# Rotary queries and keys of a two-layer decoder, produced with their dimensions on partitions

## The chip, the cores and the metric

The kernel runs on one core of one Trainium2 chip, as a single launch. The metric is the device time of that launch in microseconds. The median of three runs of the kernel before is 1182.6 us (1182.31 to 1185.84).

## The reference

Eight sequences (B) of 256 tokens (S) with 256 features (D) pass through two decoder layers, all in float32. Every layer is self-attention, cross-attention and a feed-forward network of experts, each on a layer norm of the residual stream and added back to it. Only the self-attention is touched by the change. It has 16 heads of 16 dimensions. Layer 0, cut to what matters:

```python
def _rotate_half(x):                      # layer 0: pairs of neighbours
    x1 = x[..., 0::2]
    x2 = x[..., 1::2]
    return jnp.stack((-x2, x1), axis=-1).reshape(x.shape)
...
q = (x @ Wq.T + bq).reshape(B, S, H, D).transpose(0, 2, 1, 3)
k = (x @ Wk.T + bk).reshape(B, S, H, D).transpose(0, 2, 1, 3)
v = (x @ Wv.T + bv).reshape(B, S, H, D).transpose(0, 2, 1, 3)
q = q * cos + _rotate_half(q) * sin       # _apply_rope
k = k * cos + _rotate_half(k) * sin
attn = jax.nn.softmax(jnp.einsum('bhqd,bhkd->bhqk', q, k) / SCALE, axis=-1)
out = jnp.einsum('bhqk,bhkd->bhqd', attn, v)
return out.transpose(0, 2, 1, 3).reshape(B, S, E) @ Wo.T + bo
```

Layer 1 has no biases, masks the future (causal), and its rotation exchanges the two halves of a head: dimension i goes with dimension i + 8, `concatenate([-t2, t1])`.

## The kernel before

Three stages follow one another: the attention of both layers with layer 0's experts, the projections and cross-attention of layer 1, and layer 1's experts. The change lies in the first stage alone, in the function `plain`.

That stage is a list of 24 *units*, each one attention of one sequence. Counted from 0 in the order in which they run: self-attention of sequences 0 and 1 (units 0, 1), their cross-attention (2, 3), then the same for the next two sequences, up to unit 15; units 16 to 23 are the self-attention of layer 1. The experts of layer 0 (`chosen_experts`, a generator, among it a Sinkhorn chain in which TensorE's `cs` sums alternate with short VectorE instructions) are threaded between the units.

A unit has four *steps* (k = 0 to 3). In step k TensorE makes the next scores (`Core.scores`, L326 to L360: four matmuls into the tile `st`, which fills four PSUM banks and has one buffer), ScalarE turns them into two exponential tiles `pT` (L345), in layer 1 GpSimd zeroes the future in each (`affine_select`, L350), and TensorE multiplies the exponentials of the step before with the values (`o`, L371). VectorE transposes and divides what comes out (`divided_T`, L382).

Everything a unit needs ahead of its first scores is done during the units before it. `beside(n, k, at, made)` puts a piece of work into step k of unit n, after the value products; `EARLY` puts it before them. The order on all five engines is as written (`tc.manual_schedule`), each engine taking its instructions strictly in that order. The pieces of a self-attention unit n are, with their places:

- `norm` (unit n-3, step 3, early) and `rows` (n-2, step 2): the layer norm, and its transposition to `xnT`, features on partitions.
- `heads(0)` (n-2, step 3) and `heads(1)` (n-1, step 0), L452: queries and keys of tokens 0 to 127, then of tokens 128 to 255, side by side in one PSUM tile `qk` of 128 tokens x 512 columns. `product4` (L280) splits each 128x128 stationary operand into four of 32 columns, which write to four bands of 32 partitions. `rotary` (L399) multiplies from PSUM on VectorE: `qc` by the cosine table, and in two instructions `qs`, the exchanged neighbours (or halves) by the sine table. In layer 0 GpSimd adds the rotated bias (`turned`, L457). The sum of `qc` and `qs` goes to `qkr`: for the first half on GpSimd (L459), for the second on VectorE in `joined` (L463; n-1, step 1, early).
- `vals(0)`, `vals(1)` (L465): the values, copied by ScalarE to `padv`.
- `begin` (L470; n-1, step 1): four TensorE transposes of the keys and a ScalarE copy to `kT`; four transposes of the queries to the PSUM tile `qps`, and two ScalarE copies of it with a mask each (`masked_queries`, L309) to `qm`.

The tables `cos`, `sin0`, `sin1` lie with tokens on partitions, one row per token and 16 columns. The biases of queries, keys and output lie in `bs`, one row repeated on all partitions; `turn` (L574) rotates the first two once at the start. Before the loop (L948 to L968) the first units' pieces are issued in an order of their own.

Of the kernel before, what the change touches and what calls it, by code (L numbers as in the profile page):

```python
# [39 lines left out]
P = 128  # L40
# [117 lines left out]
def plain(  # L158
# [37 lines left out]
    bs = wa.tile([P, 3, D], F32, name="bias")  # L196

    def load_bias(i, v):
        row = a[f"L0_attn_{v}"].rearrange("(o d) -> o d", o=1)
        nc.sync.dma_start(bs[:, i, :], row.to_broadcast([P, D]))  # L200

    load_bias(0, "bq")
    load_bias(1, "bk")
# [8 lines left out]
    load_bias(2, "bo")  # L212
# [186 lines left out]
    def rotary(qk, t, layer, work):  # L399

        qc = work.tile([P, 2 * H, HD], F32, tag="qc", name="qc")
        nc.vector.tensor_tensor(
            qc,
            qk.rearrange("p (h d) -> p h d", d=HD),
            cos[:, t, :].unsqueeze(1).to_broadcast([P, 2 * H, HD]),
            ALU.mult,
        )
        qs = work.tile([P, 2 * H, HD], F32, tag="qs", name="qs")
        if layer == 0:
            of = "p (h i s) -> p s h i"  # L410
            src, dst = qk.rearrange(of, s=2, i=HD // 2), qs.rearrange("p h (i s) -> p s h i", s=2)
            sn = sin0[:, t, :].rearrange("p (i s) -> p s i", s=2)
        else:
            of = "p (h s i) -> p s h i"
            src, dst = qk.rearrange(of, s=2, i=HD // 2), qs.rearrange("p h (s i) -> p s h i", s=2)
            sn = sin1[:, t, :].rearrange("p (s i) -> p s i", s=2)
        for s in range(2):
            nc.vector.tensor_tensor(
                dst[:, s],
                src[:, 1 - s],  # L420
                sn[:, s, :].unsqueeze(1).to_broadcast([P, 2 * H, HD // 2]),
                ALU.mult,
            )
        return qc.rearrange("p h d -> p (h d)"), qs.rearrange("p h d -> p (h d)")

    class SelfAttention:
# [17 lines left out]
        def rows(self):  # L444
            self.xnT = transposed(self.xn, work, mm, "xnT")
            self.qkr = work.tile([P, 2, 2 * D], F32, tag="qkr", name="qkr")
# [5 lines left out]
        def heads(self, t):  # L452
            qk = mm.tile([P, 2 * D], F32, tag="mm", name="qk")
            self.projected(qk, t, 0, 2 * D)
            qc, qs = rotary(qk, t, self.layer, work)
            if self.bias is not None:
                nc.gpsimd.tensor_tensor(qc, qc, self.bias[0][:, t, :], ALU.add)  # L457
            if not t:
                nc.gpsimd.tensor_tensor(self.qkr[:, t, :], qc, qs, ALU.add)  # L459
            self.parts = qc, qs  # L460

        def joined(self):
            nc.vector.tensor_tensor(self.qkr[:, 1, :], *self.parts, ALU.add)  # L463
# [6 lines left out]
        def begin(self):  # L470
            kT = transposed(self.qkr[:, :, D:], work, mm, "kT")
            qps = mm.tile([P, 2, S], F32, tag="mm", name="qps")
            for t in range(2):
                for c in range(2):
                    nc.tensor.transpose(qps[:, c, bass.ts(t, P)], self.qkr[:, t, bass.ts(c, P)], ident)
            qm = masked_queries(work, qps, mask2)
            mine = dens[:, 2 * self.layer, 2 * self.b : 2 * self.b + 2]
            self.core = Core(kT, qm, self.v_pad, 1.0 / math.sqrt(HD), self.layer == 1, None, mine)
# [92 lines left out]
    turned = pads.tile([P, 2, 2 * D], F32, name="turned")  # L571
    offset = pads.tile([P, D], F32, name="offset")

    def turn():  # L574
        for t in range(2):
# [393 lines left out]
    for n, u in enumerate(units):  # L969
        if n == 1:  # L970
            expert_tables()
        if n == 3:
            zeros()
# [1886 lines left out]
```

## Time and profile before

| | us |
|---|---|
| median of three runs | 1182.6 |
| the profiled execution | 1187.22 |
| its span, first to last instruction | 1185.5 |
| first scores of unit 0 begin (timeline) | 22.45 |
| scores of the last step of unit 23 begin (timeline) | 446.49 |
| mean granted TensorE clock | 0.993 |

How the clock was granted and how the engines were used in 40 equal slices of 29.6 us each stands on the page:

```profile
PE   5798899998899999999999999999999999999997
...
DVE  5555777777766633833433424242324583222213
ACT  2576665764434451323232323232413231222220
POOL 2335355454736731414141414141416214100004
PEclk8999999999999999999999999999999999999999
```

Each digit is the busy share of a slice in tenths; PEclk is the clock that TensorE was granted, in tenths of full speed. The attention units fill the first fifteen slices. Of a group of instructions the profile gives the time in which at least one of them ran, then the mean of one: four matmuls on four bands of the array run at the same time, so the first number is less than the count times the mean.

### The profile page before, as it was taken

To read this page: it belongs to the slowest core of one execution; us is meant where nothing else is said; L and a number is where in the kernel's file an instruction comes from. 1 tells how busy PE (TensorE), PEld (TensorE's weight loads), DVE (VectorE), ACT (ScalarE), POOL (GpSimd) and SP (SyncE) were. 2 spreads that over 40 slices of the span, in tenths; PEclk is the share of its full clock that TensorE was granted. 3 is DMA by queue.
4 is the path that set the end of the run, shared out by engine and by line. 5 is a ranking of instruction groups with operands and counts; after the bars stand their busy time and mean duration, and the time that the engine had idled before them with its cause. 6 is when DMAs were issued, how large, how long until landed. Compare 5 with 4: busy or idle time off the path is not lost.

```text
span 1185.5 us, 32965 instructions
## 1 busy us (share of the span) xinstructions
PE 1128.8 (95%) x14300; PEld 704.3 (59%) x14300; DVE 565.5 (48%) x1564; ACT 447.5 (38%) x696; POOL 420.9 (36%) x482
## 2 busy tenths in 40 slices
PE   5798899998899999999999999999999999999997
PEld 2344444453445454566666666666666576888864
DVE  5555777777766633833433424242324583222213
ACT  2576665764434451323232323232413231222220
POOL 2335355454736731414141414141416214100004
PEclk8999999999999999999999999999999999999999
DMA  7036233050200600010101020202012107699924
GB/s 228 1 123 217 92 107 106 10 167 1 85 2 12 223 20 3 18 38 19 38 19 41 16 51 6 55 2 55 2 37 75 36 19 319 258 411 394 404 89 140
DMA packets 51451, 116.84 MB, mean 99 GB/s; under 512 B 8273, under 2 KB 36417, under 8 KB 46945
## 3 DMA queue, kind: packets, MB, share of 16 engines
q1 hardware_dynamic: 45120, 98.90, 24.4%
q0 software_dynamic: 3456, 12.73, 3.0%
q10 hardware_dynamic: 2720, 3.02, 0.7%
q8 instruction: 114, 1.87, 0.6%
q14 instruction: 41, 0.33, 0.1%
HBM read 104.00 MB, written 27.93 MB: 111 GB/s over the span
## 4 chain that ended last, share of the span: by engine, by line
PE 76%; DVE 7%; POOL 6%; issue 6%; ACT 4%; DMA 1%; SPq 0%; POOLq 0%; ACTq 0%; DVEq 0%
PE h L276 7%; PE k L276 6%; PE v L276 6%; PE wo L276 5%; PE ox L1471 5%; PE stx L1431 5%; PE st L334 4%; PE out L1848 4%; PE out L1665 4%; PE o L371 3%; PE qk L282 3%; PE h L1079 3%; PE q L276 3%; ACT pT L345 2%; PE tr L291 2%
## 5 line engine op out<-in xcount | busy, mean ns | idle before, releaser
L345 ACT ACTIVATE pT<-st 128x1024 f32<-128x1024 f32 (+1 forms) x128 | 110.7, 920 | 65.1 <-PE st L334 63.9
L371 PE MATMUL o<-pT,padv 128*32 128x256 f32 (+1 forms) x1536 | 99.8, 370 | 4.3 <-POOL pT L350 4.2
L1437 POOL TENSOR_TENSOR both<-pTx 128x512 f32<-128x512 f32 x64 | 82.4, 1315 | 25.5 <-ACT pTx L1435 23.2
L371 PEld LDWEIGHTS o<-pT,padv 128*32 128x32 f32 x1536 | 40.6, 109 | 85.5 <-issue 38.0
L276 PE MATMUL h<-xrT,w 128*64 128x128 f32 (+1 forms) x1936 | 87.1, 250 | 1.9 <-issue 1.9
L276 PEld LDWEIGHTS h<-xrT,w 128*64 128x64 f32 x1936 | 84.3, 137 | 3.2 <-ACT yr L1857 1.0
L345 ACT ACTIVATE pT<-st,kbias 128x1024 f32<-128x1024 f32 x64 | 67.9, 1112 | 44.1 <-PE st L334 44.1
L258 POOL TENSOR_TENSOR lnrs<-lnve,mhalf 128x2 f32<-128x2 f32 x48 | 35.0, 731 | 128.1 <-DVE lnve L256 118.4
L1072 DVE TENSOR_TENSOR midr<-sl,h 128x128 f32<-128x128 f32 x102 | 29.4, 289 | 102.4 <-PE h L276 67.7
L1435 ACT ACTIVATE pTx<-stx 128x1024 f32<-128x1024 f32 x64 | 62.1, 1022 | 39.9 <-PE stx L1431 39.9
L1071 ACT ACTIVATE sl<-h 128x128 f32<-128x128 f32 (+1 forms) x114 | 35.4, 311 | 96.4 <-PE h L276 57.4
L334 PE MATMUL st<-qm,kT 32*128 32x512 f32 (+1 forms) x512 | 67.2, 594 | 3.8 <-ACT pT L345 1.8
L1431 PE MATMUL stx<-qTx,kTx 64*128 64x256 f32 x512 | 64.3, 391 | 2.5 <-ACT pTx L1435 2.5
L282 PE MATMUL qk<-l_wqkv,xnT 128*32 128x512 f32 x512 | 65.4, 624 | 0.7 <-ACT xnT L294 0.7
L1471 PE MATMUL ox<-pTx,vx 128*32 128x256 f32 x1024 | 62.4, 380 | 0.0
L1526 POOL TENSOR_TENSOR oT<-oT,rs 128x512 f32<-128x512 f32 x30 | 37.7, 1289 | 66.2 <-DMA rs<-rd 66.2
L1431 PEld LDWEIGHTS stx<-qTx,kTx 64*128 64x128 f32 x512 | 46.1, 186 | 20.8 <-ACT pTx L1435 7.2
L276 PE MATMUL wo<-wout_x,oT 128*64 128x256 f32 x512 | 58.0, 379 | 0.0
L350 POOL TENSOR_SCALAR_AFFINE_SELECT pT<-pT 128x512 f32<-128x512 f32 x64 | 42.2, 673 | 43.2 <-ACT pT L345 40.1
L258 POOL TENSOR_TENSOR lxrs<-lxve,mhalf 128x2 f32<-128x2 f32 x8 | 5.6, 706 | 133.2 <-DVE sc L1210 102.9
L387 DVE STREAM_TRANSPOSE by_q<-o 128x512 f32<-128x512 f32 x48 | 34.1, 711 | 29.8 <-PE o L371 29.6
L1848 PE MATMUL out<-w,midr 128*64 128x256 f32 x408 | 47.1, 379 | 1.1 <-issue 1.1
(361 smaller groups left out, 2159.3 us busy)
## 6 DMA issues: line engine op xcount, KB each, us to landing
w<-packs SPq DMA_DIRECT2D x22, 1408.0 KB
w<-packs SPq DMA_DIRECT2D x22, 768.0 KB
rs<-rd SPq DMA_DIRECT2D x16, 512.0 KB
packs<-L_ffn_w_eDF SPq DMA_DIRECT2D x8, 704.0 KB
packs<-L_ffn_w_eDF SPq DMA_DIRECT2D x8, 640.0 KB
packs<-L_ffn_w_eFD SPq DMA_DIRECT2D x8, 640.0 KB
ctxT<-ctx_T SPq DMA_DIRECT2D x8, 512.0 KB
wkv_x<-L_xattn_Wkv POOLq DMA_DIRECT2D x1, 4096.0 KB, 14.3
```

Of the source, the lines that this page charges most:

```text
L276: nc.tensor.matmul(out[h], lhsT[:, h], rhs, start=start, stop=stop, skip_group_check=True)
L282: nc.tensor.matmul(out[h : h + HP], lhsT[:, h : h + HP], rhs, start=start, stop=stop, skip_group_check=True)
L334: nc.tensor.matmul(st[:, r, :, :n], self.kT[rows, c, bass.ts(kt, P)], self.qm[rows, :, c, q0:], start=True, stop=True,)
L345: nc.scalar.activation(pT[:, :, :, :n], st[:, 2 * k : 2 * k + 2, :, :n], AF.Exp, scale=self.scale, **kb)
L350: nc.gpsimd.affine_select(out=pT[:, :, :, :P], in_=pT[:, :, :, :P], compare_op=ALU.is_ge, fill=0.0, base=0, pattern=[[0, 2], [0, 2], [1, P ...
L371: nc.tensor.matmul(o[HP * j : HP * j + HP, m, q0:], self.v_pad[:, kt, 8 * c + 2 * j + m, :], pTs[j // 2][:, j % 2, m, : S - q0], start=kt ...
L1431: nc.tensor.matmul(st[:, g, kt, :], kT[rows, c, bass.ts(kt, P)], qT[rows, c, :], start=True, stop=True)
L1435: nc.scalar.activation(pT, st, AF.Exp, scale=scale)
L1437: nc.gpsimd.tensor_tensor(both, pT[:, :, 0, :], pT[:, :, 1, :], ALU.add)
L1471: nc.tensor.matmul(o[at : at + HP, i, :], v[:, kt, 2 * (c2 + i) + g, lo : lo + HP], pT[:, g, kt, :], start=kt == 0, stop=kt == 1, skip_gro ...
L1665: nc.tensor.matmul(ps, mid[:, i, lo : lo + P], w2[:, i, :], start=i == 0, stop=i == NFC - 1)
L1848: nc.tensor.matmul(ps[h], mid[:, i, h], sets[k % len(sets)][1][:, i, :], start=i == 0, stop=i == NFC - 1, skip_group_check=True,)
```

## The change

Queries and keys of the self-attention are made the other way round. `heads(0)` now makes the queries of all 256 tokens and `heads(1)` the keys, with the 256 dimensions on partitions (in two halves of 128) and the tokens along the free axis: the weights are the stationary operand and `xnT` the moving one. The result needs no transposition, so `begin` keeps only the masked copies, and `kT` is what `joined` writes. `joined` moves from step 1 to step 2 of unit n-1.

The rotation takes place in that layout. The tables are widened to 128 columns by a VectorE copy (`repeated`), transposed on TensorE and copied by ScalarE (`by_dims`): `cosT` and `sinT0` before the first unit's projections, `sinT1` at the start of unit 9. The exchange of dimensions is one `stream_shuffle` on VectorE, which permutes within 32 partitions (by 1 in layer 0, by 8 in layer 1), and the sine product follows as a separate instruction: on GpSimd, except for the keys of layer 1 and of unit 0, where it is on VectorE. In layer 0 ScalarE adds the bias while it copies the projection from PSUM to SBUF (`qb`), so the biases are loaded as one number per partition, and the rotated bias is gone.

The order before the loop changes too: statistics and norm of the second unit come before the first unit's projections, both values after `begin` and `joined`.

```diff
-    load_bias(0, "bq")
-    load_bias(1, "bk")
+    bqk = wa.tile([P, 2, 2], F32, name="bqk")
+    for i, v in enumerate(("bq", "bk")):
+        nc.sync.dma_start(bqk[:, i, :], a[f"L0_attn_{v}"].rearrange("(c p) -> p c", p=P))
...
-    def rotary(qk, t, layer, work):
...
+    def repeated(src):
+        wide = work.tile([P, 2, P], F32, tag="wide", name="wide")
+        nc.vector.tensor_copy(
+            wide.rearrange("p t (h d) -> p t h d", d=HD), src.unsqueeze(2).to_broadcast([P, 2, P // HD, HD])
         )
+        return wide
+
+    def by_dims(dst, wide):
+        ps = mm.tile([P, 2, S], F32, tag="mm", name="turn")
+        for t in range(2):
+            nc.tensor.transpose(ps[:, 0, bass.ts(t, P)], wide[:, t, :], ident)
+        nc.scalar.copy(dst, ps[:, 0, :])
+
+    def rotary(src, layer, engine):
+
+        def all_heads(t):
+            return t.unsqueeze(1).to_broadcast([P, 2, S])
+
+        qc, qs = (work.tile([P, 2, S], F32, tag=n, name=n) for n in ("qc", "qs"))
+        nc.vector.tensor_tensor(qc, src, all_heads(cosT), ALU.mult)
+        step = HD // 2 if layer else 1
+        nc.vector.stream_shuffle(
+            qs.rearrange("p c t -> p (c t)"), src.rearrange("p c t -> p (c t)"), [i ^ step for i in range(HP)]
+        )
+        engine.tensor_tensor(qs, qs, all_heads(sinT1 if layer else sinT0), ALU.mult)
+        return qc, qs
...
-        def heads(self, t):
-            qk = mm.tile([P, 2 * D], F32, tag="mm", name="qk")
-            self.projected(qk, t, 0, 2 * D)
-            qc, qs = rotary(qk, t, self.layer, work)
+        def heads(self, i):
+            src = mm.tile([P, 2, S], F32, tag="mm", name="qk")
+            for f in range(2):
+                lo = i * D + f * P
+                for c in range(2):
+                    product4(src[:, f, :], self.w[:, c, lo : lo + P], self.xnT[:, c, :], c == 0, c == 1)
             if self.bias is not None:
-                nc.gpsimd.tensor_tensor(qc, qc, self.bias[0][:, t, :], ALU.add)
-            if not t:
-                nc.gpsimd.tensor_tensor(self.qkr[:, t, :], qc, qs, ALU.add)
-            self.parts = qc, qs
+                ps, src = src, work.tile([P, 2, S], F32, tag="qb", name="qb")
+                for f in range(2):
+                    nc.scalar.activation(src[:, f, :], ps[:, f, :], AF.Identity, bias=self.bias[0][:, i, f : f + 1])
+            own = i and (self.layer or not self.n)
+            self.parts = rotary(src, self.layer, nc.vector if own else nc.gpsimd)
+            if not i:
+                self.qr = work.tile([P, 2, S], F32, tag="qr", name="qr")
+                nc.gpsimd.tensor_tensor(self.qr, *self.parts, ALU.add)
 
         def joined(self):
-            nc.vector.tensor_tensor(self.qkr[:, 1, :], *self.parts, ALU.add)
+            self.core.kT = work.tile([P, 2, S], F32, tag="kT", name="kT")
+            nc.vector.tensor_tensor(self.core.kT, *self.parts, ALU.add)
...
         def begin(self):
-            kT = transposed(self.qkr[:, :, D:], work, mm, "kT")
-            qps = mm.tile([P, 2, S], F32, tag="mm", name="qps")
-            for t in range(2):
-                for c in range(2):
-                    nc.tensor.transpose(qps[:, c, bass.ts(t, P)], self.qkr[:, t, bass.ts(c, P)], ident)
-            qm = masked_queries(work, qps, mask2)
+            qm = masked_queries(work, self.qr, mask2)
...
-            beside(n - 1, 1, EARLY, u.joined)
+            beside(n - 1, 2, EARLY, u.joined)
...
     first_u.stats()
+    wides = [repeated(t) for t in (cos, sin0)]
     first_u.norm()
...
-    turn()
     first_u.rows()
+    for dst, wide in zip((cosT, sinT0), wides):
+        by_dims(dst, wide)
+    second_u.stats()
+    second_u.norm()
     first_u.heads(0)
-    second_u.stats()
-    first_u.vals(0)
     first_u.heads(1)
-    second_u.norm()
+    first_u.begin()
     first_u.joined()
-    first_u.vals(1)
+    for t in range(2):
+        first_u.vals(t)
     second_u.rows()
-    first_u.begin()
     first_u.core.scores(0)
...
+        if n == 9:
+            by_dims(sinT1, repeated(sin1))
```

## The prediction

> **What bounds the kernel now.** I read the page first: busy shares, then the chain of waits.
>
> ```profile
> PE 1128.8 (95%) x14300; PEld 704.3 (59%) x14300; DVE 565.5 (48%) x1564; ACT 447.5 (38%) x696; POOL 420.9 (36%) x482
> ...
> PE 76%; DVE 7%; POOL 6%; issue 6%; ACT 4%; DMA 1%; SPq 0%; POOLq 0%; ACTq 0%; DVEq 0%
> ```
>
> TensorE is busy nearly always, and the chain runs through it. But the edit lies only in the 24 attention units, which end near 450 us; after them every engine's instruction order is unchanged. So I read the windows of busy time there.
>
> ```profile
> 150.00:200.00 50.00, 49.43 (x766) 24.91 (x762) 37.67 (x121) 31.49 (x40) 27.37 (x30) 1.00 0.29 90
> ...
> 300.00:350.00 50.00, 45.05 (x760) 24.17 (x756) 34.36 (x110) 19.70 (x34) 26.38 (x32) 0.97 0.16 51
> ```
>
> Columns: window, length, then PE, PEld, DVE, ACT, POOL busy, clock, DMA. VectorE is at 69 to 75% and GpSimd above 50%: little room beside TensorE. How TensorE and ScalarE alternate is in the timeline of unit 9's begin step (units count from 0 in execution order; 0, 1, 4, 5, 8, 9, 12, 13 are layer 0's self-attention, 16 to 23 layer 1's).
>
> ```profile
> 156.44 1.14 PE L334 MATMUL st<-qm,kT 32*128 32x512 f32 x8
> ...
> 157.71 1.94 ACT L345 ACTIVATE pT<-st 128x1024 f32<-128x1024 f32 x2 [2.44 <-PE st L334]
> ...
> 158.51 0.75 PE L291 MATMUL tr<-ident,qkr 128*128 128x128 f32 x4
> ...
> 159.10 0.60 PE L475 MATMUL qps<-ident,qkr 128*128 128x128 f32 x4
> ...
> 159.70 1.14 PE L334 MATMUL st<-qm,kT 32*128 32x512 f32 x8
> ```
>
> The score tile has one buffer, so a step is never shorter than scores 1.14 + two exponentials 1.94 + hand-over, 3.26 us here (157.71+1.94 = 159.65, next scores 159.70); with the key bias the exponentials take 2.12, giving 3.44. TensorE work shortens a step only down to that floor. This begin step already stands on it: its eight transposes are hidden.
>
> **The change, part by part.**
>
> *Projection of queries and keys.* Both orders stream the same columns. From the groups by form:
>
> ```profile
> L282 PE MATMUL qk<-l_wqkv,xnT 128*32 128x512 f32 x512 | 65.4, 624 | 0.7 <-ACT xnT L294 0.7
> ...
> L282 PE MATMUL v<-l_wqkv,xnT 128*32 128x256 f32 x512 | 33.1, 379 | 0.0
> ...
> L291 PE MATMUL tr<-ident,qkr 128*128 128x128 f32 x64 | 11.9, 301 | 2.5 <-DVE qkr L463 2.5
> ...
> L475 PE MATMUL qps<-ident,qkr 128*128 128x128 f32 x64 | 10.2, 284 | 1.5 <-DVE ys L756 1.5
> ```
>
> The new qk has 1024 records of 256 columns, the form of v: 2 x 33.1 = 66.2 us against 65.4. Cost +0.8, twice the weight loads included, since v has that pattern.
>
> *Transposes gone.* 11.9 + 10.2 = 22.1 us of TensorE, 1.38 a unit. This is the bait; the floor decides how much is kept. Begin steps are now (us, from the timeline's score starts): unit 1 4.84, 4 3.96, 8/12/16 4.29 each, 5/9/13 3.26 each; layer 1: 17 3.53, 18 7.87, 19 4.67, 20 5.35, 21 3.72, 22 4.48, 23 3.53. Cutting each by at most 1.38 (1.58 in unit 1, where TensorE also idles 1.52 for the key sum) and not below its floor leaves 11.0 at most, not 22. What is late next takes more:
> - Unit 1: nothing else is late; keep 1.6.
> - Unit 4: ScalarE now runs the value copy (0.37) and both masked copies (1.27) straight behind the exponentials; they end at 82.3 where the next exponential began at 82.45. Keep 0.15.
> - Units 8, 12, 16: before the scores stands cs, which waits for VectorE's Sinkhorn chain. Keys reach VectorE 0.45 later (bias pass on ScalarE), the chain meets the new GpSimd product, and ends about 1.1 us after cs started before; the 0.85 is lost. Keep 0.
> - 5, 9, 13: nothing to keep.
> - 17, 18, 19, 20, 21, 22, 23: 0.3, 0.7 (VectorE's chain to cs stays; only the key sum leaves it), 1.0 and 0.4 in 19 and 21 (the causal select then ends last), 0.7 in 20, 0 in 22, 0.3 in 23: 3.4.
>
> *Rotation.* VectorE before: per unit 2 x (0.69 + 2 x 0.415) + 0.69 = 3.73 us. After, with a shuffle taken as 0.71 (nearest row: STREAM_TRANSPOSE by_q, 128x512, 711 ns; between 0.6 and 0.9), layer 0: 2 x (0.69 + 0.71) + 0.69 = 3.49; layer 1 adds the key's sine product, 0.69: 4.18. A shift of -0.2 and +0.45 a unit, beside TensorE. If the shuffle took 1.4, that cover would go: 32 x 0.7 = 22 us, part of it on the cs chains.
>
> GpSimd: in layer 0 two sine products replace two bias sums, 1.28 each: neutral. In layer 1 one product of 1.28 is added in front of the query sum, and behind both in the queue stand the causal selects and picks that TensorE waits for:
>
> ```profile
> 409.00 1.27 POOL L459 TENSOR_TENSOR qkr<-qc,qs 128x512 f32<-128x512 f32 x1
> ...
> 410.24 1.68 POOL L350 TENSOR_SCALAR_AFFINE_SELECT pT<-pT 128x512 f32<-128x512 f32 x2
> ...
> 411.98 0.52 PE L371 MATMUL o<-pT,padv 128*32 128x128 f32 x10 [0.55 <-POOL pT L350]
> ```
>
> There the wait grows by 1.28 and eats unit 22's 1.2. Near 423.8 the select has 2 us of slack, kept. At 314.25 two picks stand behind the query sum and TensorE already waits for them (1.07 at 315.24): I charge 1.3. At 366.25 likewise 0.7, already in unit 20's value. Layer 1 nets 3.4 - 1.3 = 2.1.
>
> *A rule that speaks against the change.* The row first:
>
> ```profile
> 339.04 1.28 POOL L459 TENSOR_TENSOR qkr<-qc,qs 128x512 f32<-128x512 f32 x1 [2.82 <-DVE qs L418]
> ...
> 339.16 1.21 DVE L662 TENSOR_TENSOR g<-g,rc 128x32 f32<-128x32 f32 x1
> ```
>
> A 0.19 us product took 1.21, ending with GpSimd's sum. The Trainium skill, "SBUF — State Buffer", section "Who interferes with whom", says why: a VectorE instruction with two SBUF inputs and a GpSimd instruction reading SBUF exclude each other for a whole instruction. In layer 0 the cosine product now reads the biased copy in SBUF instead of PSUM, so it joins that class. By the rule at its worst, all 16 cosine products lose a GpSimd instruction of 1.28: 20 us of VectorE. By the trace, GpSimd is idle or between instructions when most of them would start (135.4, 140.2, 93.8); I take 0.3 each, 5 us, beside TensorE except in the cs chains, where it is already charged.
>
> *ScalarE.* Four bias passes of 128x256 per layer-0 unit, 0.38 each by the padv row (379 ns): 12.2 us; the kT copies (16 x 0.59 = 9.4) go. They fall behind projections that TensorE follows with 1.14 us of scores, so exponentials don't wait. No activation table load is added.
>
> *Opening.* Now:
>
> ```profile
> 18.80 0.68 DVE L463 TENSOR_TENSOR qkr<-qc,qs 128x512 f32<-128x512 f32 x1
> ...
> 20.04 1.06 PE L475 MATMUL qps<-ident,qkr 128*128 128x128 f32 x4
> ...
> 21.13 1.27 ACT L313 ACTIVATE qm<-qps,mask 128x512 f32<-128x512 f32 x2 [0.27 <-PE qps L475]
> 22.45 2.09 PE L334 MATMUL st<-qm,kT 32*128 32x512 f32 x8 [1.36 <-ACT qm L313]
> ```
>
> After: turning the biases (eight VectorE instructions, 8.0 to 12.0) goes; two table copies (0.25 each) enter the statistics and wait for the table loads, which land at 6.6 and 6.85: first normalisation 1.0 late. Four table transposes cost 1.1 on the cold array: queries start near 11.1, end 13.6, biased 14.1, cosine and shuffle 15.65, sine and sum on GpSimd 18.25, masks 19.6. First scores at 19.65, gain 2.8. TensorE meanwhile has the keys, both values and the second rows, so its clock, granted at half near 19 to 26 (scores 2.09, not 1.14), should stay up: 1.3 more. Together 4.1; between 0 (clock drops again, bias gathers of 4-byte elements late) and 5.
>
> SP's queue keeps its number and order of DMAs: two bias gathers stand where two broadcast rows stood, ahead of x(1), which lands at 8.1 and is read near 9.
>
> *Table for layer 1.* Two transposes stand before unit 9's second scores and wait for a VectorE copy queued behind attT, which ends at 167.66; the scores that began at 166.76 would start near 168.4: cost 1.6, once.
>
> **Sum.** 4.1 + 1.6 + 0.15 + 2.1 - 1.6 = 6.35 gained; less 0.15 for later exponentials in 5, 9, 13: 6.2. Against its own run, 1187.2 us (span 1185.5 and 1.7 around it): 1181.0. That run stood 4.6 over the median of the runs, 1182.6; the same gain there gives **1176.4**.
>
> **Rivals.**
> 1. *TensorE bound all along*: all 22.1 kept, minus 0.8 and 1.0 for six table transposes, plus 4.1: gain 24, 1158. For it: PE 95%. Against: three begin steps at the floor. 7%.
> 2. *The transposes were hidden and the opening's gain does not come*: -6.2 + 4.1 and some stalls: 1181 to 1184, no change. For it: the steps of 3.26. 18%.
> 3. *GpSimd's queue becomes the bound* (slower): if the extra 1.28 in front of selects and picks reaches TensorE in six layer-1 units (7.7) and the port exclusion adds 1.1 to each of six cs steps (6.6), with the 6.2 gained: net +8, 1190. It decides once GpSimd's waits exceed the 6.2, five late selects. For it: selects already late at 291, 402 and 412. Against: slack of 2 us elsewhere. 20%.
> The rotation not being what is claimed is not open: shuffle by 1 or 8 within 32 rows swaps the pairs.
>
> **Numbers.** Faster by my sum 55%, rival 1 7%, rival 2 18%, rival 3 20%. What a measurement can tell from no change is 0.3%, 3.5 us; my sum's own spread (1170 to 1181) crosses that a little. Faster 0.59, same 0.19, slower 0.22. The range takes the opening's and the shuffle's bounds and most of rival 3: 1165 to 1189; the likeliest case alone, 1170 to 1181.
>
> **What would show it.** Right: first scores near 19.7; begin steps of 5, 9, 13 unchanged near 3.3, unit 1's about 3.3; TensorE busy some 20 us less while the span falls by a third of that; a stall near 168. Wrong: STREAM_SHUFFLE well over 0.71; TensorE's waits for GpSimd's selects over 10 us in total; half clock after the first scores.

## The result, and the profile after

| | before | after |
|---|---|---|
| median of four runs, one chip | 1183.3 us | 1191.07 us (1190.07 to 1192.51) |
| the profiled execution | 1187.22 | 1192.51 |
| its span | 1185.5 | 1190.8 |
| first scores of unit 0 begin | 22.45 | 20.78 |
| scores of the last step of unit 23 begin | 446.49 | 450.64 |

The ratio is 1.0058 (95% interval 1.0040 to 1.0076): slower by 0.6%, some 6.9 us, where 6.2 us of gain were forecast. In a later set of runs the same kernel gave 1.0059 (1.0037 to 1.0082). The prediction was wrong in its sign.

The page of the changed kernel, busy shares and chain of waits:

```profile
PE 1116.2 (94%) x14690; PEld 710.7 (60%) x14690; DVE 576.7 (48%) x1568; ACT 454.2 (38%) x715; POOL 430.6 (36%) x489
...
PE 73%; POOL 8%; DVE 7%; issue 6%; ACT 4%; DMA 0%; SPq 0%; POOLq 0%; ACTq 0%; DVEq 0%
```

TensorE does 12.6 us less, and the span is 5.3 longer. GpSimd's share of the chain went from 6% to 8%. The groups by form show that the new instructions cost about what they were priced at (mean ns behind the comma after the bar):

```profile
L278 PE MATMUL qk<-xnT,l_wqkv 128*32 128x256 f32 x1024 | 65.2, 394 | 0.8 <-issue 0.8
...
L414 DVE TENSOR_TENSOR qc<-qb,cosT 128x512 f32<-128x512 f32 x16 | 12.0, 750 | 21.6 <-ACT qb L456 21.6
...
L416 DVE STREAM_SHUFFLE qs<-qb 128x512 f32<-128x512 f32 x16 | 11.8, 739 | 0.0
```

TensorE's busy time fell, though by less than the 20 of the forecast, so the loss is one of waits, or of the clock. To find them I took, from the timeline, the time from each step's first score matmul to the next one's. I call such a stretch by unit and step: 18.2 runs from the start of unit 18's scores of step 2 to those of step 3. The begin step of unit 19 is 18.2. Summed over parts, in us, with the two profiles (minus is a gain):

| part | forecast | measured | where it lies |
|---|---|---|---|
| opening to the end of unit 3 | -5.85 | -3.32 | first scores -1.67, 0.0 -0.22, 0.2 -1.58, 0.3 +0.50, 1.2 +0.12, 3.2 -0.52 |
| units 4 to 15 | +1.75 | +3.36 | 9.0 +1.71; 8.3 and 12.3 +0.71 each; 7.1, 7.2, 11.1, 11.2, 15.1 together +1.0; 15.2 -0.85 |
| layer 1 | -2.1 | +4.12 | 16.1 to 16.3 +0.66, 17.1 +1.32, 18.0 +0.68, 18.2 -1.42, 18.3 +1.62, 19.2 +0.21, 20.2 -0.46, 20.3 +1.61, 21.0 +1.36, 21.2 -1.15, 22.2 -0.27 |
| all that follows | 0 | +1.1 | within the spread: this part took 737 to 744 us in the profiles of the kernels below that leave it as it is |

The begin steps 0.2, 3.2, 15.2, 18.2, 20.2, 21.2 and 22.2 are all shorter, as the missing transposes let one expect, and those of units 5, 9 and 13 are unchanged at 3.26. Those of units 8 and 12 (7.2, 11.2) are longer. What was not expected stands right behind them. This is the timeline of the changed kernel at 18.2 and 18.3, TensorE first, then GpSimd (start, duration, engine; in brackets the idle time before and what ended it):

```profile
354.52 0.71 PE L330 MATMUL st<-qm,kT 32*128 32x256 f32 x8 [0.68 <-ACT pT L341]
355.95 1.61 PE L367 MATMUL o<-pT,padv 128*32 128x256 f32 x14 [0.72 <-POOL pT L346]
...
359.73 0.44 PE L287 MATMUL tr<-ident,xn 128*128 128x128 f32 x2 [0.72 <-POOL xn L258]
360.10 1.14 PE L330 MATMUL st<-qm,kT 32*128 32x512 f32 x8
```

```profile
354.57 0.72 POOL L254 TENSOR_TENSOR lnrs<-lnve,mhalf 128x2 f32<-128x2 f32 x1 [7.75 <-DVE lnve L252]
355.25 1.42 POOL L346 TENSOR_SCALAR_AFFINE_SELECT pT<-pT 128x512 f32<-128x512 f32 x2
356.68 3.00 POOL L258 TENSOR_SCALAR xn<-x,lnmv,lnrs 128x256 f32<-128x256 f32 x2
```

In the kernel before, TensorE at 18.3 had no such wait in brackets, and GpSimd's norm was shorter:

```profile
354.39 2.43 POOL L262 TENSOR_SCALAR xn<-x,lnmv,lnrs 128x256 f32<-128x256 f32 x2
```

The scores of 18.3 start 1.4 us sooner after those of 18.2, and TensorE then waits for a select and again for the norm `xn`. GpSimd's chain of root, selects and norm hangs on VectorE's statistics, and none of it has anything to do with the transposes. Before the change 18.2 and 18.3 took 4.68 + 3.96 = 8.64 together, now 3.26 + 5.58 = 8.84.

A caution for reading single profiles: some stretches change by 1 to 2 us from one execution of the same kernel to the next. The changed kernel, run again, had 5.59 instead of 4.41 in 0.0, 9.06 instead of 7.38 in 16.1 and 10.81 instead of 9.59 in 17.1. The granted clock goes with it: 16.1 had 1.00 in the first run and 0.81 in the second, 17.1 had 1.00 and 0.92. In the kernel before, 16.1 took 9.10 at 0.81. So the +0.66 of 16.1 to 16.3 in the table hides a longer delay; beside a profile of the old layout that had 1.00 there (15.68, the kernel before with the shorter chain below), the changed kernel's 17.48 is 1.80 more. The +1.36 of 21.0 also stands beside a lower clock (0.79, before 1.00), and the key sum moved in layer 1, below, had 6.70 there at 1.00, as before the change. I use such stretches only where several kernels agree.

### The profile page after: what moved, and what is told of

It is laid out like the page before. It is cut to its first block, busy times and chain, and to the rows that moved or that the text cites. A ratio compares the mean times of both kernels' runs of the same rounds, so it can differ in the third digit from the quotient of the medians.

```text
span 1190.8 us, 33765 instructions
## 1 busy us (share of the span) xinstructions
PE 1116.2 (94%) x14690; PEld 710.7 (60%) x14690; DVE 576.7 (48%) x1568; ACT 454.2 (38%) x715; POOL 430.6 (36%) x489
## 4 chain that ended last, share of the span: by engine, by line
PE 73%; POOL 8%; DVE 7%; issue 6%; ACT 4%; DMA 0%; SPq 0%; POOLq 0%; ACTq 0%; DVEq 0%
PE h L272 7%; PE k L272 6%; PE v L272 6%; PE wo L272 5%; PE ox L1467 5%; PE stx L1427 5%; PE out L1844 4%; PE st L330 4%; PE out L1661 4%; PE h L1075 3%; PE q L272 3%; PE o L367 3%; PE qk L278 3%; POOL xn L258 2%; ACT pT L341 2%
## 5 line engine op out<-in xcount | busy, mean ns | idle before, releaser
L278 PE MATMUL qk<-xnT,l_wqkv 128*32 128x256 f32 x1024 | 65.2, 394 | 0.8 <-issue 0.8
L1522 POOL TENSOR_TENSOR oT<-oT,rs 128x512 f32<-128x512 f32 x30 | 37.8, 1291 | 65.2 <-DMA rs<-rd 65.2
```

The source lines that it names most:

```text
L278: nc.tensor.matmul(out[h : h + HP], lhsT[:, h : h + HP], rhs, start=start, stop=stop, skip_group_check=True)
```

## The experiments

Theories: **give-back** (mine, after the result: what the transposes freed is returned a step later, to waits for GpSimd's norm and select chain), **queue** (rival 3: the added product on GpSimd delays what stands behind it), **placement** (the table's turn and the keys of layer 0 come late). Each ratio is to the kernel before on the same chip, with its 95% interval.

### What the transposes alone are worth

```diff
-            kT = transposed(self.qkr[:, :, D:], work, mm, "kT")
...
-            qm = masked_queries(work, qps, mask2)
+            kT, qm = self.qkr[:, :, D:], masked_queries(work, self.qkr[:, :, :D], mask2)
```

> The kernel before with one part left out: the eight transposes and the kT copy of every self-attention; the masked copies and the scores read the untransposed rows (so the attention's values are others). It measures what 22 us of TensorE are worth here, alone. Give-back theory (the transposes stood beside other waits; where TensorE gains, it waits in the next step for GpSimd's norm and selects): begin steps 4, 5, 8, 9, 12, 13 gain at most 0.5, unit 1 about 1.6, opening 1.5 to 2.5, layer 1's gains of 1.4 in units 19 and 0.5 in 21 come back within a step; net 4 to 7, 1176 to 1179. Queue theory (all of the loss is the extra product on GpSimd, which this kernel doesn't have): the floors' 11.0 plus the opening are kept, 1170 to 1172. TensorE bound: 1159 to 1161.

The other values of the attention send this kernel through a routine for rare inputs at its end, so its total (1307.83 us) says nothing, and only its attention stage is read. There the last scores begin 5.2 us earlier than before (4.6 of it by the end of unit 15): within the 4 to 7 of the give-back theory, far from 22, but not term by term. Units 8 and 12 gained more than the 0.5 at most that I had expected, and the opening gained 0.5 where I had expected 1.5 to 2.5. The begin stretches gain what the floors allow: 1.58, 0.52, 0.85 three times, then in layer 1 0.27, 1.42, 1.03, 0.46, 1.03 and 0.27, together 9.1. Layer 0 keeps its part. In layer 1, 4.5 us are gained and 4.3 lost in the next stretches: 16.3 +0.83, 18.3 +2.58, 20.3 +0.89. (16.1 -1.77 and 17.3 +1.23 stand beside that; they are of those that vary with the clock. About 1 us of the 2.58 is the clock too: this profile had a clock of 0.50 from 350 to 352, and 14 matmuls of `ao` took 2.15 there, in the changed kernel at a clock of 1.00 they took 1.24.) At 18.3, in that kernel's timeline:

```profile
349.29 2.27 PE L371 MATMUL o<-pT,padv 128*32 128x256 f32 x14 [1.08 <-POOL pT L350]
```

No part of the new rotation is in this kernel, so a give-back is shown for the transposes alone; its size without the lower clock is about 3.3 of the 4.5 us.

### The product on GpSimd, taken out and put in

```diff
-            own = i and (self.layer or not self.n)
+            own = self.layer or (i and not self.n)
```

> The changed kernel, with the sine product of layer 1's queries on VectorE too: 1.28 off GpSimd in each of eight units, 0.69 more on VectorE. Queue theory (rival 3: the extra product in front of selects and picks): the 7.7 us of layer 1 come back, 1183 to 1184. Give-back theory: only the two late picks and selects that stand right behind that product (unit 16's steps 2 and 3, unit 17's step 1) come back, 2.5 to 3.5: 1187.5 to 1188.5; the losses of units 18 and 20 (last steps) stay. Placement theory (turn of the table, late keys): no change, 1191.

Measured: 1.0014 (1.0003 to 1.0026). From 1.0058 that is 5.2 us back: between the two theories, nearer to neither. As the give-back theory had it, the long 18.3 and 20.3 stay (5.57 and 5.16), so they don't come from this product. Then the opposite edit, in the kernel before, with a sum of the same size in the product's place:

```diff
+            elif not t:
+                spare = work.tile([P, 2 * D], F32, tag="spare", name="spare")
+                nc.gpsimd.tensor_tensor(spare, qc, qs, ALU.add)
```

> The kernel before with one more GpSimd product of 128x512 in front of the query sum of every layer-1 unit (its result is not used): rival 3's price alone, without any other part of the change. Queue theory as I wrote it (1.28 in six units): 7 to 8 us more. By the trace of the changed kernel: only where GpSimd has no slack behind it, unit 16's steps 2 and 3, unit 17's step 1, unit 19's step 2 and unit 21's step 2: 3 to 5 us. If GpSimd has slack everywhere: 0 to 1.

Measured: 1.0046 (1.0029 to 1.0063), 5.5 us more. Two opposite edits in two kernels give the same size: the work added on GpSimd costs about 5.3 us, instead of the 7.7 that rival 3 wrote. The clearest place is 17.1, where TensorE's `rps` (rows for the experts) needs the `pick` tiles that GpSimd makes. First the timeline of the kernel before with the extra sum (called `spare`), GpSimd and TensorE; then TensorE in the kernel before, in the changed kernel, and in the one with that product on VectorE:

```profile
309.61 1.27 POOL L460 TENSOR_TENSOR spare<-qc,qs 128x512 f32<-128x512 f32 x1
310.84 1.28 POOL L462 TENSOR_TENSOR qkr<-qc,qs 128x512 f32<-128x512 f32 x1
312.07 1.23 POOL L350 TENSOR_SCALAR_AFFINE_SELECT pT<-pT 128x512 f32<-128x512 f32 x2
313.30 1.83 POOL L712 TENSOR_SCALAR pick<-idx_row,tokid 128x256 f32<-128x256 f32 x2
...
314.28 3.69 PE L282 MATMUL rps<-pick,xnb 128*32 128x256 f32 x32 [2.30 <-POOL pick L712]
```

```profile
315.24 0.64 PE L282 MATMUL rps<-pick,xnb 128*32 128x256 f32 x8 [1.07 <-POOL pick L709]
```

```profile
317.28 0.64 PE L278 MATMUL rps<-pick,xnb 128*32 128x256 f32 x8 [1.35 <-POOL pick L701]
```

```profile
312.55 0.64 PE L278 MATMUL rps<-pick,xnb 128*32 128x256 f32 x8
```

GpSimd runs there without a gap, so its queue length is what TensorE waits for: 2.30 with the extra sum, 1.07 before, 1.35 in the changed kernel, nothing there with the product gone. In the first of these timelines the long wait is followed by `rps` at about half speed (3.69, with a clock of 0.57 granted from 314 to 318; with the product on VectorE the 32 matmuls take 2.39, from 312.55 to 314.94), which is why one instruction of 1.27 costs 2.56 in that stretch. Over 16.1 to 16.3 the same product costs 1.06 (16.74 against 15.68 in the kernel before with another edit further on), in 19.2 1.22.

Not all of it is queue. At 18.0 the second GpSimd instruction in a row holds up VectorE, as in the row of the prediction from this same place. The second of two Sinkhorn products `g` and the sum `cs` in the kernel before (no wait, so no bracket), then in the changed one:

```profile
340.83 0.19 DVE L668 TENSOR_TENSOR g<-g,rr 128x32 f32<-128x32 f32 x1
...
341.17 0.32 PE L282 MATMUL cs<-g,ones 128*32 128x16 f32 x16
```

```profile
342.80 0.88 DVE L660 TENSOR_TENSOR g<-g,rr 128x32 f32<-128x32 f32 x1
...
343.83 0.32 PE L278 MATMUL cs<-g,ones 128*32 128x16 f32 x16 [0.78 <-DVE g L660]
```

GpSimd's sum runs from 342.37 to 343.64, and `g` ends with it. This is the +0.68 of 18.0. The extra sum in the kernel before has it too (0.76 for `g`, a wait of 0.67). With the product on VectorE 18.0 stays long, at 9.84: the sine product then stands in VectorE's own queue ahead of `g`.

### Placement

The key sum of layer 1 back at the head of step 1:

> The changed kernel with the key sum of layer 1 alone back at the head of step 1, where it stood before. Give-back theory with the port: the norm on GpSimd beside it in units 18 and 20, last step, returns from 3.00 and 2.86 to 2.43: 0.5 to 1.0 us, 1190 to 1190.5; the other part of the loss there (1.1 each) stays since GpSimd's chain is the end. Queue theory and placement theory (layer 0): no change.

Measured: 1.0070 (1.0048 to 1.0092): no gain. 18.3 fell from 5.58 to 5.37, and 19.2 rose from 5.56 to 6.06. In the changed kernel the norm beside the moved key sum takes 3.00 us against 2.43 before, but moving the sum away buys nothing that six runs show. The widening copy of the table one unit earlier:

```diff
+        if n == 8:
+            wide1 = repeated(sin1)
         if n == 9:
-            by_dims(sinT1, repeated(sin1))
+            by_dims(sinT1, wide1)
```

> The changed kernel with the widening copy of the layer-1 sine table issued one unit earlier (unit 8) and its two transposes where they are. Placement theory: the 1.5 us of TensorE's wait at the head of unit 9 go, and with them nothing else comes in their place: 1189.4 to 1189.7. Give-back theory: the same at this place. Queue theory: up to 0.3, since a later chain absorbs it.

Measured: 1.0035 (1.0017 to 1.0054), and 9.0 fell from 4.98 to 3.31, 1.67 where 1.5 was expected; the ratios put it at 2.7 with a wide margin. Two lines of the changed kernel's TensorE show that wait (second line), and the one for the keys that stands 4.6 us ahead of it:

```profile
161.35 1.14 PE L330 MATMUL st<-qm,kT 32*128 32x512 f32 x8 [0.64 <-DVE kT L465]
...
165.99 0.41 PE L405 MATMUL turn<-ident,wide 128*128 128x128 f32 x2 [1.47 <-DVE wide L397]
```

Both moves with a third, layer 0's key sum at the end of step 1:

```diff
-            beside(n - 1, 2, EARLY, u.joined)
+            beside(n - 1, *((2, EARLY) if u.layer else (1, 65)), u.joined)
```

> The changed kernel with three moves: layer 1's query sine product on VectorE, the sine table widened one unit earlier, and the key sum of layer 0 made in step 1 behind the masked copies instead of at the head of step 2 (there it stood behind a run of MAX8 instructions and the scores of units 9 and 13 waited 0.7 each for it). If the losses add up as the trace of the changed kernel has them: 5.2 + 1.7 + 1.4 = 8.3 less than the changed kernel, a ratio to the kernel before of 0.998 to 0.999. If the gains are one and the same slack: 1.001, as the sine product's move alone.

Measured: 0.9987 (0.9976 to 0.9998), as the sum of the losses had it. 8.3 and 12.3 are back at 3.80. The key sum on VectorE in the changed kernel, between two MAX8 instructions (they serve the experts' choice), then in this one, ahead of them:

```profile
160.53 0.67 DVE L465 TENSOR_TENSOR kT<-qc,qs 128x512 f32<-128x512 f32 x1
161.13 0.41 DVE L672 MAX8 top<-v 16x8 f32<-16x256 f32 x1
```

```profile
155.62 0.69 DVE L465 TENSOR_TENSOR kT<-qc,qs 128x512 f32<-128x512 f32 x1
```

### GpSimd's norm chain

If that chain is what took the gain, shortening it should pay more in the new kernel than in the old one.

```diff
-                    self.xn[:, t, :], x[:, 2 * self.b + t, :], self.mv, self.rs, t, nc.gpsimd if self.n > 1 else nc.vector
+                    self.xn[:, t, :], x[:, 2 * self.b + t, :], self.mv, self.rs, t, nc.gpsimd if 1 < self.n < 16 else nc.vector
```

> The three moves, and the layer norm of layer 1's units on VectorE instead of GpSimd (2.43 us off GpSimd's queue in each unit, some 0.8 more on VectorE). Give-back theory (where the transposes went, TensorE now waits for GpSimd's chain of root, selects and norm in the next step): the last steps of units 16, 18 and 20, now 1.6, 1.6 and 1.2 longer than before the change, get most of that back: 2 to 4 us under the three moves. If what ends that wait is the selects or VectorE's statistics, no gain, 0 to 0.5, or a loss, as VectorE then waits for GpSimd's root at the head of its queue.

> The kernel before with that same move of layer 1's norm to VectorE, and nothing else. Give-back theory: before the change the transposes cover GpSimd's chain, so the move is worth less here than in the changed kernel: 0 to 1.5 us. If it is worth as much (2 to 4), that wait has nothing to do with the transposes.

Measured: 1.0026 (1.0015 to 1.0037) and 1.0025 (1.0012 to 1.0038). Both are losses, against 0.9987 and 1, and neither gave what I had expected of the give-back theory. The first kernel's timeline shows one of the places, 18.3, VectorE and then TensorE:

```profile
353.00 1.35 DVE L258 TENSOR_SCALAR xn<-x,lnmv,lnrs 128x256 f32<-128x256 f32 x2 [0.84 <-POOL lnrs L254]
354.27 0.70 DVE L383 STREAM_TRANSPOSE by_q<-o 128x512 f32<-128x512 f32 x1
```

```profile
355.12 1.20 PE L367 MATMUL o<-pT,padv 128*32 128x256 f32 x16 [2.21 <-DVE by_q L383]
```

VectorE waits at the head of its queue for GpSimd's root; behind it stands `by_q`, which empties the only `o` tile, and TensorE waits for that. Moving the norm puts the wait on a busier engine. The same stands at 15.0, where VectorE waits 0.90 for the root and TensorE's `cs` then 2.64 (1.16 with the three moves alone); 15.0 and 15.1 are 1.5 longer each in both kernels. A gentler edit, for units 20 and 22: statistics ahead of a run of MAX8, the root behind the selects (that part of the edit is not shown), half of the norm on VectorE behind the division.

```diff
-                beside(n - 2, 0, 80, u.stats)
+                beside(n - 2, 0, 65, u.stats)
                 beside(n - 2, 1, EARLY, u.norm)
+                beside(n - 2, 1, 1, u.norm_half)
```

> The three moves, and for units 20 and 22 alone a shorter chain from the statistics to the transposed norm: the statistics stand ahead of a run of MAX8 instructions, GpSimd takes the root behind the causal selects instead of ahead of them, and the second half of the norm is made on VectorE behind the division of the step. Give-back theory: the last steps of units 18 and 20, which took 5.59 and 5.33 under the three moves (3.96 before the change), lose the waits of TensorE for select and norm there, 1.4 and 1.2: 2.2 to 2.8 us under the three moves, ratio 0.996 to 0.997. If TensorE's wait there comes from something else: 0 to 0.5.

> The kernel before with that same shorter chain in units 20 and 22 and nothing else. Give-back theory: with the transposes in place that chain ends while TensorE still works, so nothing is to be had: last steps of units 18 and 20 unchanged within 0.3, ratio 0.9995 to 1.0005. If the chain is worth as much here (2.2 to 2.8), then it was not the transposes that covered it.

Measured: 0.9985 (0.9975 to 0.9995) with the three moves, 0.9979 (0.9969 to 0.9990) in the kernel before. The stretches moved as expected in the first: 18.3 from 5.59 to 4.24, 20.3 from 5.33 to 3.31, but 19.2 rose by 1.20, and no gain over the three moves shows in the medians, where 2.2 to 2.8 us were expected. In the kernel before I had expected nothing, and 18.3 and 20.3 fell too, from 3.96 to 3.10 and 3.21. So the chain held TensorE there already before the change. The trace had it, inside a group instead of in a bracket. TensorE at 18.3 in the kernel before, then in the same with the shorter chain:

```profile
353.92 1.35 PE L371 MATMUL o<-pT,padv 128*32 128x256 f32 x14
...
356.29 1.02 PE L291 MATMUL tr<-ident,xn 128*128 128x128 f32 x4
```

```profile
350.90 1.07 PE L375 MATMUL o<-pT,padv 128*32 128x256 f32 x16
...
352.76 0.66 PE L295 MATMUL tr<-ident,xn 128*128 128x128 f32 x4
```

The same 16 matmuls (in the first row 14 of them, the other two begin at 355.11) and four transposes take 1.07 and 0.66 when nothing holds them. The rows of 1.35 and 1.02 held short waits. There was no slack behind unit 19's begin step, and I could have read that. So the part of the theory by which the transposes had covered the chain in full is wrong; what stands is that the chain's end, and not the transposes, set the start of the next scores.

### Layer 0's bias pass

```diff
-            if self.bias is not None:
+            if False:
                 ps, src = src, work.tile([P, 2, S], F32, tag="qb", name="qb")
```

> The changed kernel without the bias pass of layer 0: the rotation reads the projection in PSUM, and the bias of queries and keys is left out (it is all zeros in these inputs). It takes 0.84 us per projection off ScalarE, brings queries and keys 0.5 to 0.8 earlier to VectorE, and takes the 16 cosine products out of the class that GpSimd can exclude. If the bias pass holds the keys back ahead of the Sinkhorn sums: units 8, 12, 16 keep up to 0.85 each and the small losses there (0.9 in sum) go: 2 to 3.5 us less, 1188 to 1189. If the sums wait for other things: 0 to 0.5.

Measured: 1.0016 (1.0001 to 1.0031). 7.2 fell from 4.51 to 3.62 and 11.2 from 4.61 to 3.71, at the places where the Sinkhorn sum `cs` stands ahead of the scores. The total is 5 us better. These two hold 1.8 of that, and 8.3 and 12.3 fell by 0.27 each; the rest is not placed. Two edits asked by what means the pass costs this: in the first the pass runs but nobody reads it, in the second the cosine product alone reads PSUM. (Their steps 30 and 46 are 7.2 and 11.2.)

> The changed kernel, with the bias pass on ScalarE kept but not used: the rotation reads the projection in PSUM (the bias of layer 0's queries and keys, all zeros here, is left out). If ScalarE's own time was the cost, this stays with the changed kernel, steps 30 and 46 at 4.5 to 4.6, 1.005 to 1.006. If the delay of the data or the port was it, it goes with the kernel without the pass: steps 30 and 46 at 3.6 to 3.7, some 2.5 us less.

> The changed kernel, with the cosine product alone reading the projection in PSUM and the shuffle still reading the biased copy (the bias of the cosine part, all zeros here, is left out). Port theory (VectorE products of two SBUF inputs excluded by GpSimd, 6.6 us in rival 3): steps 30 and 46 fall to 3.6 to 3.7 as without the pass. Delay theory (the biased copy comes late for the shuffle, and so do the sine product, the key sum and the Sinkhorn chain behind them): at most half of that, 4.1 to 4.6.

Measured: 1.0039 (1.0025 to 1.0054) and 1.0034 (1.0024 to 1.0044); 7.2 is 4.51 in both. (By the ratios both are 2 to 3 us faster than the changed kernel, with intervals that overlap; 7.2 and 11.2 don't give that.) VectorE's line in the second kernel:

```profile
134.68 0.69 DVE L414 TENSOR_TENSOR qc<-qk,cosT 128x512 f32<-128x512 f32 x1 [1.09 <-ACT qb L457]
```

The product reads PSUM and runs its undisturbed 0.69, yet it starts only after the pass, which reads the same PSUM tile. The Trainium skill, "PSUM — Partial Sum Buffer", section "PSUM bank collisions raise a hardware error", has a rule that fits: ScalarE and VectorE may not access one bank of a partition at the same time, two reads included, so a program has to set them one behind the other. No run here shows that this rule, and no other, set the order. So these two say that the cosine product's port is not the cause, since 7.2 stays at 4.51 with a product that has one SBUF input. They don't separate ScalarE's time from the delay, because the delay was still in both. The exponentials of the changed kernel speak against ScalarE's time: at 7.2 they begin at 137.85, and their scores end at 136.59 + 1.14 = 137.73. What is left is the delay: VectorE idles 1.08 for the biased copy, and the Sinkhorn chain stands behind it. In the changed kernel:

```profile
137.27 0.69 DVE L414 TENSOR_TENSOR qc<-qb,cosT 128x512 f32<-128x512 f32 x1 [1.08 <-ACT qb L456]
...
138.80 1.24 DVE L654 TENSOR_TENSOR g<-g,rc 128x32 f32<-128x32 f32 x1
```

```profile
140.84 0.32 PE L278 MATMUL cs<-g,ones 128*32 128x16 f32 x16 [1.25 <-DVE g L660]
```

The long `g` is a rival: without its 1.05 us beside GpSimd's sine product the sum would come earlier too. But it is as long in the kernel without the pass, where the cosine product waits only 0.21, for its projection, and TensorE 0.36:

```profile
135.22 1.23 DVE L654 TENSOR_TENSOR g<-g,rc 128x32 f32<-128x32 f32 x1
...
137.26 0.32 PE L278 MATMUL cs<-g,ones 128*32 128x16 f32 x16 [0.36 <-DVE g L660]
```

So the 0.9 between the two kernels is the later copy (1.08 - 0.21 = 0.87), and the long `g` is a cost that both pay.

### A version that beats both

The three moves, the shorter chain, and layer 0's keys without the pass: the bias is added inside the products that VectorE makes from PSUM, with a bias shuffled once for the sine part.

```diff
+            for f in range(2):
+                nc.vector.scalar_tensor_tensor(qc[:, f, :], src[:, f, :], bias[0][:, f : f + 1], cosT, ALU.add, ALU.mult)
...
+            for f in range(2):
+                engine.scalar_tensor_tensor(qs[:, f, :], qs[:, f, :], bias[1][:, f : f + 1], sinT0, ALU.add, ALU.mult)
```

> The three moves and the shorter chain, and in layer 0 the keys' bias added inside the two VectorE products instead of in a pass on ScalarE (four products of 128x256 that each add the bias and multiply by the table; the sine product so leaves GpSimd too). The keys reach VectorE 0.5 to 0.8 sooner ahead of the Sinkhorn sums. If the bias pass is what held units 8 and 12 back: steps 30 and 46 (counted over all units) fall from 4.5 to 3.6, 2 to 2.5 us under the shorter chain: ratio 0.996 to 0.997. If VectorE's extra 0.8 a unit takes that place: 0.9985 or above.

Measured: 1179.62 us beside 1185.71, 0.9941 (0.9920 to 0.9963): faster than the kernel before by 0.6%, and by the two ratios than the changed kernel by about 1.2%. That is more than the 0.996 to 0.997 that I had expected; 7.2 and 11.2 hold 1.6 us of the 5.2 by which its ratio lies under that of the shorter chain, and the rest is not placed. 7.2 is 3.72 and 11.2 3.81. Its busy shares and its `cs` at the end of 7.2:

```profile
PE 1114.2 (94%) x14690; PEld 710.9 (60%) x14690; DVE 584.3 (49%) x1603; ACT 447.2 (38%) x699; POOL 407.0 (34%) x472
```

```profile
141.92 0.32 PE L282 MATMUL cs<-g,ones 128*32 128x16 f32 x16 [0.47 <-DVE g L682]
```

TensorE does as much as in the changed kernel; GpSimd does 23.6 us less, VectorE 7.6 more. The layout of the change is kept throughout; what differs is where a few pieces stand and which engine makes them.

The changed kernel once more, as a control on the chip of the shorter-chain runs:

> The changed kernel itself on this chip, so that the differences of the edits can be read against it: by its first runs 1.0058 of the kernel before (1.0040 to 1.0076), all theories.

Measured: 1193.16 us, 1.0059 (1.0037 to 1.0082).

## Why the prediction was wrong, point by point

The step that failed is the netting of layer 1, "3.4 - 1.3 = 2.1" gained, which measured 4.1 lost. It put at nothing what the step behind a shortened begin step takes back, which was 3.2 us at 18.3 and 20.3, most of it there without the new product too (5.57 and 5.16). And it charged the new product on GpSimd 3.2 us (unit 22's 1.2, 1.3, and 0.7 in unit 20), which cost about 5.3. Outside layer 1 the later key sum of layer 0, put at nothing too, took 1.4. With the product, layer 0's key sum and the table's copy moved, the kernel came from 1.0058 to 0.9987 (8.4 us, where the three single losses add up to 8.3).

- **TensorE's floor, and 11.0 of the 22.1 us at most**: right. With the transposes alone gone, the begin stretches gained 9.1 and the attention 5.2; steps of 3.26 stayed. The new `qk` matmuls took 65.2 us (66.2 forecast), the shuffle 0.74 (0.71).
- **"What is late next takes more", layer 1 nets 3.4 - 1.3 = 2.1**: this step failed. I asked what is late next inside the begin step, not in the step after it. Units 19 and 21 gained 1.42 and 0.46 in their begin steps (1.0 and 0.4 forecast), and 18.3 and 20.3 took back 1.62 and 1.61. At 20.3 that is more than was gained; 0.4 of it goes with the product (5.16 without it), the rest is not placed. Unit 18, priced at 0.7, gained nothing in its begin step (17.2), and unit 20, priced at 0.7 too, lost 0.21; unit 22, priced at 0, gained 1.15, beside 1.36 lost in 21.0. Without the transposes, and nothing else changed, layer 1 as a whole gained 0.6.
- **"There the wait grows by 1.28 and eats unit 22's 1.2 ... I charge 1.3"**: the other failure, a cost too small and in part in the wrong place. The product on GpSimd cost 5.2 us when removed and 5.5 when added by itself. I had found three places where selects or picks stand behind it. Another lies at 16.2 and 16.3, where GpSimd has no gap from 289.7 to 307.2 and the delay runs through selects and two norms; at 19.2 it cost 1.0 to 1.2 where I had charged 0.7. In 17.1 the product's place was right, and half-speed matmuls behind the longer wait, which some of the profiles have, were not priced. Nor was 18.0.
- **Rival 3, 1190**: the time came true and its first half did, at 5.3 us for 7.7. Its second half did not: "the port exclusion adds 1.1 to each of six cs steps" (6.6) is at most 1.7 in all: 1.0 over 7.1, 7.2, 11.1, 11.2 and 15.1, and 0.7 at 18.0. That the sum met 1191 is luck in part: both its losses were smaller, and so were the gains that it set against them. Though it had 20%, its own 1190 lay outside my range, which ended at 1189.
- **The port rule and the cosine product**: I took 5 us on VectorE, the rule at its worst 20; the product averages 0.750 where it reads SBUF and 0.683 where it reads PSUM, so 16 x 0.067 = 1.1, of which 0.9 is a single product in the opening that took 1.61 beside GpSimd's sine product. The rule of the Trainium skill, "SBUF — State Buffer", section "Who interferes with whom", bit elsewhere: the Sinkhorn products `g` average 0.447 us, up from 0.359, some of them 1.24 beside GpSimd's 1.28.
- **Units 8, 12, 16 "keep 0"**: right for 8 and 12, and slightly less than nothing came (+0.44 over 7.1 and 7.2, and as much over 11.1 and 11.2). Wrong for 16, which has no bias in layer 1 and kept 0.85. Both causes named are in the traces: the biased copy, 0.87 later at 7.2 where I had "0.45", and the new GpSimd product, beside which `g` took 1.24 (0.55 before).
- **Units 1 and 4, "keep 1.6" and "keep 0.15"**: their begin steps gained 1.58 and 0.52. Behind unit 1's, 0.3 took back 0.50 (0.30 in the second run). For unit 4 I had added up ScalarE's durations (2.12 + 0.37 + 1.27 and hand-over, 3.84), but consecutive ones overlap by 0.1, and from one exponential to the next it was 3.50 (75.64 to 79.14).
- **"5, 9, 13: nothing to keep"**: right for their begin steps, but the key sum moved behind MAX8 instructions and units 9 and 13 lost 0.7 each in the stretch after. The move of `joined` was in the diff, and I priced it nowhere.
- **The turn of the table, 1.6**: right, 1.71.
- **The opening, 4.1**: 2.8 of it for the first scores, the rest for the clock. In the changed kernel the biased queries were ready at 14.87 (14.1 forecast) and GpSimd's query sum at 19.37 (18.25). The first scores begin at 20.4 on average over eight profiles with this opening and at 22.4 over four with the old one: 2.0. The 1.3 for the clock was a misreading, as the last section shows.
- **VectorE and ScalarE beside TensorE**: right in that no exponential of the changed kernel waits for a bias pass. Their busy times rose by 11.2 and 6.7 us, more than my pieces give (7 with the port's 5, and 2.8); a bias pass takes 0.47 on average instead of 0.38.

## What to carry to other kernels

A gain in one step is only worth what the next wait leaves: follow the freed engine to its next two or three waits, and treat a group that takes longer than its like as a wait that is already there. When work moves onto an engine that executes in order, look for stretches where that engine has no gap; there added work reaches whoever waits for its last instruction, even if its busy share is 36%. When a piece is made later, or on another engine, name what stands ahead of it in its new place.

## What the hardware showed beyond that

The clock after the first scores differs between executions of one kernel. The window from 19 to 23 us (length, then busy time of PE, PEld, DVE, ACT, POOL; the granted clock is the number before the last two) in the kernel before, in the kernel before with the shorter chain, and in the changed kernel and its second run:

```profile
19.00:23.00 4.00, 2.64 (x15) 2.09 (x18) 0.48 (x1) 2.44 (x4) 0.00 (x0) 0.53 1.08 365
```

```profile
19.00:23.00 4.00, 2.34 (x17) 1.57 (x20) 1.12 (x3) 2.34 (x4) 0.05 (x1) 1.00 1.07 371
```

```profile
19.00:23.00 4.00, 2.22 (x12) 0.71 (x16) 1.60 (x2) 2.41 (x6) 0.36 (x1) 0.69 1.07 371
```

```profile
19.00:23.00 4.00, 2.76 (x16) 0.92 (x20) 1.06 (x2) 2.81 (x6) 0.00 (x0) 0.56 1.06 369
```

The same at 16.1, in the kernel before and in the changed one:

```profile
288.66:297.76 9.10, 7.33 (x65) 2.55 (x61) 6.86 (x20) 1.08 (x2) 8.54 (x10) 0.81 0.00 0
```

```profile
288.71:296.09 7.38, 5.65 (x81) 2.73 (x77) 6.78 (x20) 1.08 (x2) 6.74 (x8) 1.00 0.00 0
```

After the first scores the two kernels with the old opening had 0.53 and 1.00, with the same instructions there. The new opening had both kinds too (stretch 0.0 took 3.20 to 5.59; the changed kernel's own two runs 4.41 and 5.59). Each of the four has an idle TensorE of over 1 us just before. I had read one profile's half clock as a cost of the old order that a new one would avoid. Over the twelve profiles counted above, 0.0 took 3.9 on average with the old opening and 4.7 with the new one, so no gain shows. The Trainium skill, "TensorE: Matmul & The Clock Gate", section "What's actually happening", says that the clock is granted by activity in windows of 3.4 us that run freely, without regard to the kernel's start. That would make it a draw from one execution to the next, which agrees with these rows; the runs here show that the clock differs, not by what rule.
